# Rotary step of an attention kernel: one VectorE shuffle in place of four ScalarE copies

## The chip, the cores and the metric

The kernel runs on one core of a Trainium2 chip. The metric is the device time of one execution in microseconds (us). The core has five engines that run their own queues in order and wait for each other on semaphores: TensorE (PE in the profile, PEld its weight loads), VectorE (DVE), ScalarE (ACT), GpSimd (POOL) and SyncE (SP, which here only issues DMAs). Matmul results land in PSUM, in eight banks per partition; everything else lies in SBUF, 128 partitions wide.

## What is computed

A block with attention and a gated feed-forward part, in float32, for 4 sequences of 512 tokens and 1024 features. Cut to what the change touches, with the layer norm ahead of it:

```python
xn = _layernorm(x)
q = (xn @ Wq).reshape(b, s, 16, 64);  k = ...Wk;  v = ...Wv

def _rotate_every_two(x):
    r = jnp.stack((x[..., 1::2], x[..., ::2]), axis=-1)
    return r.reshape(x.shape)

def _apply_rotary(x, sin, cos):
    sin = jnp.repeat(sin[None, :, None, :], 2, axis=3)
    cos = jnp.repeat(cos[None, :, None, :], 2, axis=3)
    return x * cos + _rotate_every_two(x) * sin

logits = einsum(rotary(q), rotary(k)); causal mask; / sqrt(64); softmax; @ v; @ Wo
out = x + attention(xn) * silu(gated_ffn(xn))
```

The rotary step takes each pair of neighbouring features (2i, 2i+1), multiplies each by a cosine that the two share, and adds its partner times a sine that the two share. Both terms have a plus sign.

## The kernel before

The work goes by sequence b (0 to 3) and, within one, by group g (0 to 3) of four heads; a group has two units i of two heads each. Projections of queries and keys (m = 0, 1) for a group are made transposed, [128 partitions = two heads x 64 features, 512 tokens], by Strassen's scheme on halves: seven products of quarter matrices instead of eight. Each product is four matmuls of 128x256 into half a PSUM bank; `project_qk` collects them with ScalarE copies out of PSUM (L358, L387), VectorE sums out of PSUM (`add`, L352; the wide sum L389) and one GpSimd sum (L388). The result of a unit is the tile `c`. Values (m = 2) are projected by `project_v` (L425, L446, L451).

`rotary` (L313) is called one or two keys later, from inside the next projection. The host has sorted the columns of the weights so that, within a head, the 32 even features come first and the 32 odd ones after (L1388); the partner of partition p is then p + 32 or p - 32, in another block of 32 partitions. Four ScalarE copies (L319, L320) move the blocks to the tile `sw`, scaled by 0.125 for queries; VectorE makes `rot = c * sc * cos` (L321); GpSimd multiplies `sw` by the sine (L322) and adds the two (L323).

A group's attention is interleaved with the projections of the next group. `scores` (L525) writes two score tiles into a PSUM pool of their own and one (i = 1) into two banks of the shared ring; `softmax` adds the mask (L545), takes maxima (L548) on VectorE, exponentials on ScalarE (L551), reciprocals on VectorE (L559) and scales on GpSimd (L561). `transpose_blocks` transposes 32x32 blocks on VectorE (L579) and puts them in place with 16 DMAs from SyncE (L589). `values` multiplies by the values (L604), and ScalarE copies the result out of its bank (L613), which SyncE stores (L617).

The next sequence is loaded (`load_x`, L161), normalized on VectorE (L171 to L187), and transposed on TensorE: `transpose_x` makes two halves for each 128 tokens, and each half is copied out of PSUM by VectorE (L204) or ScalarE (L206). VectorE forms sums and differences of weights and of x for Strassen's scheme (`form_w` L288, `form_x` L303 and L311).

The ring is a PSUM pool of four banks that projections, the score tile i = 1, the values' products and the transposes of x share; a bank is free again when ScalarE or VectorE has read it out. The order of TensorE is the program's own, written out by hand; the order on the other engines is made by a planner from its own costs, in program order only where the code pins it. Behind the projections (from about 780 us) come the output projection (L1240) and the feed-forward part (L1011, L1180), which the change doesn't touch.

Of the kernel before, what the change touches and what calls it, by code (L numbers as in the profile page):

```python
# [11 lines left out]
AF = mybir.ActivationFunctionType  # L12
ALU = mybir.AluOpType
# [7 lines left out]
B, S, E = 4, 512, 1024  # L21
H, D = 16, 64
NE = 8
P = 128
# [4 lines left out]
TPB = S // P  # L29
# [4 lines left out]
SCALE = 0.125  # L34
# [2 lines left out]

QCOL = [0, P, 3 * P, 6 * P]
OFF = [0, 128, 256, 224]


@with_exitstack
def attn_gated_ffn_kernel(
# [15 lines left out]
    nc = tc.nc  # L59
# [13 lines left out]
        out=mask,  # L73
# [23 lines left out]
    for sign, base in ((1, 0), (-1, 7)):  # L97
        nc.gpsimd.affine_select(
            out=high,
# [42 lines left out]
    cos_sb = tabs.tile([P, S], F32, name="cos_sb")  # L142
    sin_sb = tabs.tile([P, S], F32, name="sin_sb")

    def bank(name):
        return ring.tile([P, S], F32, tag="r", name=name)

    def tp_bank(name):
        return bank(name).rearrange("p (t q) -> p t q", t=TPB)
# [44 lines left out]
    def transpose_x(b, t, g):  # L194
        if b not in X:
            X[b] = xp.tile([P, NC, S], F32, tag="X", name=f"X_{b}")
        tp = tp_bank(f"xtp_{b}_{t}_{g}")
        for j in range(4):
            c = 4 * g + j
            nc.tensor.transpose(tp[:, j, :], xin[b, t][:, c * P : (c + 1) * P], ident)  # L200
        dst = X[b][:, 4 * g : 4 * g + 4, t * P : (t + 1) * P]

        if (g == 0 and b > 0) or (g == 1 and (b, t) == (0, TPB - 1)):
            nc.vector.tensor_copy(dst, tp)  # L204
        else:
            nc.scalar.copy(dst, tp)  # L206
        if g == 1:

            queue = nc.scalar if (b, t) == (B - 1, TPB - 1) else nc.sync
            queue.dma_start(  # L210
                out=xn_d[b, t].rearrange("p (c q) -> p c q", c=NC),
                in_=X[b][:, :, t * P : (t + 1) * P],
            )
# [43 lines left out]
    def quarters_w(key):  # L257
        if key[2] < 2:
            w = W[key]
            return w[:, 0, :4, :], w[:, 0, 4:, :], w[:, 1, :4, :], w[:, 1, 4:, :]  # L260
        w, v = W[key, 0], W[key, 1]
        return w[:, :4, :], w[:, 4:, :], v[:, :4, :], v[:, 4:, :]

    def quarters_x(b):
        t = X[b]
        return t[:, :4, :TH], t[:, :4, TH:], t[:, 4:, :TH], t[:, 4:, TH:]
# [45 lines left out]

    def rotary(u, m, c):  # L313

        sc = SCALE if m == 0 else 1.0
        rot = qk.tile([P, S], F32, tag=f"rot{m}", name="rot%d_%d_%d_%d" % (m, *u))
        sw = tmp.tile([P, S], F32, tag="sw", name="sw%d_%d_%d_%d" % (m, *u))
        for r in range(0, P, 64):
            nc.scalar.activation(sw[r : r + 32, :], c[r + 32 : r + 64, :], AF.Copy, scale=sc)  # L319
            nc.scalar.activation(sw[r + 32 : r + 64, :], c[r : r + 32, :], AF.Copy, scale=sc)  # L320
        nc.vector.scalar_tensor_tensor(rot, c, sc, cos_sb, op0=ALU.mult, op1=ALU.mult)  # L321
        nc.gpsimd.tensor_tensor(sw, sw, sin_sb, op=ALU.mult)  # L322
        nc.gpsimd.tensor_tensor(rot, rot, sw, op=ALU.add)  # L323
        (Q, K)[m][u] = rot

    def project_qk(key):

        b, g, m = key
        pos = keys.index(key)
        after = keys[pos + 1] if pos + 1 < len(keys) else None  # L330
        a11, a12, a21, a22 = quarters_w(key)
        b11, b12, b21, b22 = quarters_x(b)
        un = "%d_%d_%d" % key
        c = [tmp.tile([P, S], F32, tag="c", name=f"c_{un}_{i}") for i in range(2)]

        def product(ps, wq, xq):
            for k in range(4):
                nc.tensor.matmul(  # L338
                    ps, lhsT=wq[:, k, :], rhs=xq[:, k, :], start=(k == 0), stop=(k == 3)
                )  # L340
                yield

        def halves(n):

            ps = bank(f"pj_{un}_{n}")
            return ps, ps[:, :TH], ps[:, TH:]

        def part(n):
            return tmp.tile([P, TH], F32, tag=f"part{n}", name=f"part_{un}_{n}", bufs=1)

        def add(out, ps, x):
            nc.vector.tensor_tensor(out, ps, x, op=ALU.add)  # L352

        _, p, r = halves(1)
        yield from product(p, a11, b11)
        yield from product(r, a12, b21)
        p1 = tmp.tile([P, S], F32, tag="part1", name=f"part_{un}_1", bufs=1)[:, :TH]
        nc.scalar.copy(p1, p)  # L358
        add(c[0][:, :TH], r, p1)
        if turn:  # L360
            rotary(*turn.pop(0))
        _, p, r = halves(2)
        yield from product(r, SF[key, 3], TF[b, 3])
        if pos == 0:

            bank3 = halves(3)
            yield from product(bank3[2], SF[key, 1], TF[b, 1])
        yield from product(p, SF[key, 2], TF[b, 2])
        u2, u3 = part(2), part(3)
        add(u2, p, p1)  # L370
        add(u3, r, u2)
        if turn:
            rotary(*turn.pop(0))
        if after:
            form_w(after, 3)
        if pos:
            ps, p, r = halves(3)
            yield from product(r, SF[key, 1], TF[b, 1])
        else:
            ps, p, r = bank3  # L380
        if after:
            form_w(after, 1)
            if after[2] < 2:
                form_w(after, 2)
        yield from product(p, a22, TF[b, 4])
        p5 = tmp.tile([P, S], F32, tag="part1", name=f"part_{un}_5", bufs=1)[:, :TH]
        nc.scalar.copy(p5, r)  # L387
        nc.gpsimd.tensor_tensor(u2, u2, p5, op=ALU.add)  # L388
        nc.vector.tensor_tensor(  # L389
            c[1].rearrange("p (h n) -> p h n", h=2),  # L390
            ps.rearrange("p (h n) -> p h n", h=2),
            u3[:, None, :].to_broadcast((P, 2, TH)),
            op=ALU.add,
        )
        load_w()
        _, p, _ = halves(4)
        yield from product(p, SF[key, 4], b22)
        add(c[0][:, TH:], p, u2)
        if after and after[2] < 2:
            form_w(after, 4)  # L400

        turn.extend([((b, g, i), m, c[i]) for i in range(2)])
        if m == 0:
            rotary(*turn.pop(0))
# [164 lines left out]
    def transpose_blocks(u, queues=(nc.sync,), ordered=False):  # L569
# [4 lines left out]
        for j in range(TPB):  # L574
            for i in range(j, TPB):
                src = probs(u, i)[:, :, j * P : (j + 1) * P]
                o = OFF[j] + 32 * (i - j)
                tc.keep_in_program_order(
# [17 lines left out]
    def values(u):  # L596
# [3 lines left out]
        for j in range(TPB):  # L600
            for h in range(2):
                r = h * D
                o = 320 * h + OFF[j]
                nc.tensor.matmul(  # L604
# [285 lines left out]
    for k, (b, g) in enumerate(groups):  # L890
# [38 lines left out]
        if k in (5, 9, 12, 14):  # L929
            n = {5: 0, 9: 2, 12: 4, 14: 6}[k]  # L930
# [121 lines left out]
    w, v = late  # L1052
# [318 lines left out]
def _rotary_tables():  # L1371
    f = np.float32
    inv = (f(1.0) / (f(10000.0) ** (np.arange(0, D, 2, dtype=f) / f(D)))).astype(f)
    ang = (np.arange(S, dtype=f)[None, :] * inv[:, None]).astype(f)
    return np.tile(np.cos(ang), (4, 1)).astype(f), np.tile(np.sin(ang), (4, 1)).astype(f)


# [49 lines left out]
```

## Time and profile before

| | |
|---|---|
| runs | 1107.7, 1110.0, 1110.5 us; median 1110.0 |
| span of the profiled execution | 1108.7 us, 15895 instructions |
| mean granted TensorE clock | 0.996 of full speed |
| ScalarE copies of the rotary step, L319 and L320 | 256, 628 ns each, 160.7 us |
| VectorE product L321 | 64, 734 ns mean, 45.3 us |
| GpSimd product and sum, L322 and L323 | 64 each, 1330 and 1419 ns mean |

A line of the timeline gives start and length in us, engine, line, operation, output and input tiles, how many alike in a row, and in brackets how long the engine had been idle before it and what it waited for. A line of a group gives busy us and the mean ns of one, then idle time before it and what ended that. "TensorE waits for ScalarE" means that its next matmul was released by a ScalarE instruction. Ends of matmuls are modelled, so neighbours overlap a little. The busy share by 40 slices of the span:

```
PE   9999999999999999999999999999999999999997
DVE  7888888788988978888887887887776877567663
ACT  2452754453375445427544452655530223122220
POOL 0772645555264555526453562675552433432334
```

### The profile page before, as it was taken

How to read it: one execution, taken by the hardware profiler on the slowest of the kernel's cores; microseconds unless marked ns; L12 is line 12 of the kernel's file. 1: busy time of each engine (PE TensorE's matmuls, PEld its weight loads, DVE VectorE, ACT ScalarE, POOL GpSimd, SP SyncE). 2: the span in 40 equal slices, each digit the busy share in tenths (PEclk: the TensorE clock that was granted, in tenths of full speed). 3: DMA queues.
4: the chain of work that ended last, by engine and by line, in shares of the span. 5: the costliest groups of instructions: out<-in, count | busy, mean ns of one | idle time of the engine just before them, and what ended most of it. 6: DMA issues, size and time to landing. Idle time of an engine off the chain costs nothing. (4 is left out here: it accounts for less than half of the span.)

```text
span 1108.7 us, 15895 instructions
## 1 busy us (share of the span) xinstructions
PE 1087.4 (98%) x5176; PEld 790.2 (71%) x5176; DVE 870.4 (79%) x1740; ACT 461.3 (42%) x1072; POOL 518.9 (47%) x566
## 2 busy tenths in 40 slices
PE   9999999999999999999999999999999999999997
PEld 8887778777777877777788687777664545654663
DVE  7888888788988978888887887887776877567663
ACT  2452754453375445427544452655530223122220
POOL 0772645555264555526453562675552433432334
PEclk9999999999999999999999999999999999999999
DMA  9415566544556654455666445544664222431331
GB/s 323 135 69 147 149 184 189 160 137 119 166 155 187 190 154 135 121 163 158 184 183 219 140 148 142 153 125 122 179 193 171 90 93 102 148 119 54 136 114 57
DMA packets 86770, 163.88 MB, mean 148 GB/s; under 512 B 13472, under 2 KB 49056, under 8 KB 80672
## 3 DMA queue, kind: packets, MB, share of 16 engines
q1 hardware_dynamic: 80144, 152.25, 46.1%
q0 software_dynamic: 4832, 9.05, 2.4%
q10 hardware_dynamic: 1712, 1.57, 0.5%
q8 instruction: 41, 0.67, 0.3%
q14 instruction: 41, 0.34, 0.1%
HBM read 95.45 MB, written 25.43 MB: 109 GB/s over the span
## 5 line engine op out<-in xcount | busy, mean ns | idle before, releaser
L561 POOL TENSOR_SCALAR p<-p,rs 128x256 f32<-128x256 f32 (+3 forms) x256 | 183.7, 734 | 200.6 <-DVE rs L559 136.2
L551 ACT ACTIVATE p<-sc,nmx 128x256 f32<-128x256 f32 (+3 forms) x256 | 132.9, 529 | 104.8 <-DVE nmx L548 87.2
L338 PE MATMUL pj<-X,w 128*128 128x256 f32 x576 | 134.3, 382 | 1.7 <-ACT p L551 1.5
L338 PE MATMUL pj<-T,S 128*128 128x256 f32 x512 | 120.5, 385 | 8.5 <-ACT v L613 8.5
L579 DVE STREAM_TRANSPOSE y<-p 128x256 f32<-128x256 f32 x320 | 112.4, 409 | 18.3 <-POOL p L561 16.9
L322 POOL TENSOR_TENSOR sw<-sw,sin_sb 128x512 f32<-128x512 f32 x64 | 85.1, 1330 | 81.1 <-ACT sw L320 75.4
L338 PEld LDWEIGHTS pj<-X,w 128*128 128x128 f32 x576 | 108.1, 190 | 20.0 <-issue 2.9
L338 PEld LDWEIGHTS pj<-T,S 128*128 128x128 f32 x512 | 96.7, 192 | 24.8 <-ACT v L613 11.3
L319 ACT ACTIVATE sw<-c 32x512 f32<-32x512 f32 x128 | 80.3, 628 | 70.0 <-DVE c L352 68.2
L338 PE MATMUL pj<-T,w 128*128 128x256 f32 x448 | 106.6, 382 | 0.0
L548 DVE TENSOR_REDUCE nmx<-sc 128x1 f32<-128x256 f32 (+3 forms) x160 | 105.2, 683 | 1.3
L425 PE MATMUL pj<-w,X 128*128 128x256 f32 x416 | 94.6, 380 | 0.8 <-ACT p L551 0.5
L338 PEld LDWEIGHTS pj<-T,w 128*128 128x128 f32 x448 | 83.4, 190 | 15.5 <-issue 4.6
L323 POOL TENSOR_TENSOR rot<-rot,sw 128x512 f32<-128x512 f32 x64 | 90.8, 1419 | 5.0
L425 PEld LDWEIGHTS pj<-w,X 128*128 128x128 f32 x416 | 78.2, 190 | 12.7 <-ACT p L551 2.0
L545 DVE TENSOR_TENSOR sc<-sc,mask 128x256 f32<-128x256 f32 (+1 forms) x160 | 57.0, 371 | 35.3 <-PE sc L525 35.3
L320 ACT ACTIVATE sw<-c 32x512 f32<-32x512 f32 x128 | 80.4, 628 | 1.6
L425 PE MATMUL pj<-w,T 128*128 128x256 f32 x352 | 80.2, 381 | 0.0
L525 PE MATMUL sc<-rot,rot 64*128 64x128 f32 (+3 forms) x512 | 79.7, 443 | 0.3 <-DVE v L451 0.3
L604 PE MATMUL pv<-p,v 128*64 128x256 f32 (+3 forms) x512 | 76.0, 439 | 0.4 <-issue 0.4
L388 POOL TENSOR_TENSOR part<-part,part 128x256 f32<-128x256 f32 x32 | 24.7, 771 | 105.2 <-ACT part L387 102.0
L613 ACT COPY v<-pv 128x512 f32<-128x512 f32 x32 | 18.7, 585 | 131.5 <-PE pv L604 131.4
(177 smaller groups left out, 1956.9 us busy)
## 6 DMA issues: line engine op xcount, KB each, us to landing
p<-y SPq DMA_DIRECT2D x496, 80.0 KB, 2.1
w<-in_wqk SPq DMA_DIRECT2D x31, 1024.0 KB, 5.3
w<-in_wv SPq DMA_DIRECT2D x16, 1024.0 KB, 5.2
x<-in_x SPq DMA_DIRECT2D x16, 512.0 KB, 4.3
at_d<-v SPq DMA_DIRECT2D x32, 256.0 KB, 2.7
xp<-xn_d SPq DMA_DIRECT2D x16, 512.0 KB, 4.6
ap<-at_d SPq DMA_DIRECT2D x16, 512.0 KB, 5.1
xr<-in_x SPq DMA_DIRECT2D x32, 256.0 KB, 3.0
```

The source lines that it names most:

```text
L319: nc.scalar.activation(sw[r : r + 32, :], c[r + 32 : r + 64, :], AF.Copy, scale=sc)
L320: nc.scalar.activation(sw[r + 32 : r + 64, :], c[r : r + 32, :], AF.Copy, scale=sc)
L322: nc.gpsimd.tensor_tensor(sw, sw, sin_sb, op=ALU.mult)
L323: nc.gpsimd.tensor_tensor(rot, rot, sw, op=ALU.add)
L338: nc.tensor.matmul(ps, lhsT=wq[:, k, :], rhs=xq[:, k, :], start=(k == 0), stop=(k == 3))
L425: nc.tensor.matmul(ps[:, j, :], lhsT=xq[:, k, j * P : (j + 1) * P], rhs=wq[:, k, :], start=(k == 0), stop=(k == 3),)
L525: nc.tensor.matmul(head(i, h), lhsT=Q[u][r : r + D, i * P : (i + 1) * P], rhs=K[u][r : r + D, : (i + 1) * P], start=True, stop=True,)
L548: nc.vector.tensor_reduce(nmx[:, hs], v, AX.X, ALU.max, negate=True)
L551: nc.scalar.activation(pt[:, h, :], ps[h], AF.Exp, bias=nmx[:, h : h + 1], accum_out=ssum[:, h : h + 1],)
L561: nc.gpsimd.tensor_scalar(pt[:, h, :], pt[:, h, :], rs[:, h : h + 1], 1.0, op0=ALU.mult, op1=ALU.mult,)
L579: nc.vector.transpose(out[:, :, :, o : o + 32], src.rearrange("p h (b c) -> p h b c", b=4))
L604: nc.tensor.matmul(by_block[r : r + D, :, 32 * j :], lhsT=V[u][:, j, r : r + D], rhs=PT[u][:, :, o : o + 32 * (TPB - j)], start=(j == 0), ...
```

## The change

The host no longer sorts the weights' columns: the partners lie in neighbouring partitions, 2i and 2i+1, and the tables of cosine and sine repeat each row twice. One VectorE `stream_shuffle` swaps neighbours within each block of 32 partitions, in place of the four ScalarE copies. The factor 0.125 of the queries is no longer applied in `rotary` but where the products are collected: the two ScalarE copies and the five VectorE sums of a query key take it along, and the plain product remains for the cosine. The first half of each transposed x tile of the sequences 1 to 3 is copied out of PSUM by ScalarE instead of VectorE.

```diff
+NEIGHBOUR = [n ^ 1 for n in range(32)]
...
-        if (g == 0 and b > 0) or (g == 1 and (b, t) == (0, TPB - 1)):
+        if g == 1 and (b, t) == (0, TPB - 1):
             nc.vector.tensor_copy(dst, tp)
         else:
             nc.scalar.copy(dst, tp)
...
     def rotary(u, m, c):
-        sc = SCALE if m == 0 else 1.0
...
-        for r in range(0, P, 64):
-            nc.scalar.activation(sw[r : r + 32, :], c[r + 32 : r + 64, :], AF.Copy, scale=sc)
-            nc.scalar.activation(sw[r + 32 : r + 64, :], c[r : r + 32, :], AF.Copy, scale=sc)
-        nc.vector.scalar_tensor_tensor(rot, c, sc, cos_sb, op0=ALU.mult, op1=ALU.mult)
+        nc.vector.stream_shuffle(sw, c, NEIGHBOUR)
+        nc.vector.tensor_tensor(rot, c, cos_sb, op=ALU.mult)
         nc.gpsimd.tensor_tensor(sw, sw, sin_sb, op=ALU.mult)
         nc.gpsimd.tensor_tensor(rot, rot, sw, op=ALU.add)
...
+        sc = SCALE if m == 0 else 1.0
+        def scaled_copy(out, ps):
+            if m == 0:
+                nc.scalar.activation(out, ps, AF.Copy, scale=sc)
+            else:
+                nc.scalar.copy(out, ps)
         def add(out, ps, x):
-            nc.vector.tensor_tensor(out, ps, x, op=ALU.add)
+            if m == 0:
+                nc.vector.scalar_tensor_tensor(out, ps, sc, x, op0=ALU.mult, op1=ALU.add)
+            else:
+                nc.vector.tensor_tensor(out, ps, x, op=ALU.add)
...
-        nc.scalar.copy(p1, p)
+        scaled_copy(p1, p)
...
-        nc.scalar.copy(p5, r)
+        scaled_copy(p5, r)
         nc.gpsimd.tensor_tensor(u2, u2, p5, op=ALU.add)
-        nc.vector.tensor_tensor(
+        add(
             c[1].rearrange("p (h n) -> p h n", h=2),
             ps.rearrange("p (h n) -> p h n", h=2),
             u3[:, None, :].to_broadcast((P, 2, TH)),
-            op=ALU.add,
         )
...
-    return np.tile(np.cos(ang), (4, 1)).astype(f), np.tile(np.sin(ang), (4, 1)).astype(f)
+    ang = np.tile(np.repeat(ang, 2, axis=0), (2, 1))
+    return np.cos(ang).astype(f), np.sin(ang).astype(f)
...
-        w = w.reshape(E, H, D // 2, 2).transpose(0, 1, 3, 2).reshape(E, E)
```

## The prediction

> **What bounds the kernel now.** I read the engines' busy times first, then who waits for whom, then the timelines around TensorE's waits, and last the groups that the edits touch.
>
> ```profile
> PE 1087.4 (98%) x5176; PEld 790.2 (71%) x5176; DVE 870.4 (79%) x1740; ACT 461.3 (42%) x1072; POOL 518.9 (47%) x566
> ```
>
> TensorE (PE) is busy in 1087.4 of 1108.7 us. The diff touches no matmul, and in the built changed program TensorE's instructions stand in the same order, so only the 21.3 us without a matmul, and stretches at a lowered clock, can move. Some of the 21.3 us are the start (1.5 us before the first matmul) and the tail behind the last one. In the middle, the waits view has for TensorE:
>
> ```profile
> PE pj L338 <- ACT v L613: 8.5, 7, 2.3
> ...
> PE pj L338 <- ACT p L551: 1.5, 2, 1.1
> PE pj L425 <- ACT p L551: 0.5, 1, 0.5
> ```
>
> Seven times, 8.5 us together, a projection waits for a PSUM bank that ScalarE has still to copy out (L613, the copy behind the values' matmuls). TensorE's timeline has them at 135.6, 233.5, 329.4, 427.1, 523.7, 623.5 and 720.6 us; three of the rows (start, length, what, in brackets the idle time before):
>
> ```profile
> 135.56 2.43 PE L338 MATMUL pj<-T,S 128*128 128x256 f32 x10 [1.20 <-ACT v L613]
> ...
> 427.07 3.72 PE L338 MATMUL pj<-T,S 128*128 128x256 f32 x16 [0.18 <-ACT v L613]
> ...
> 623.50 5.41 PE L338 MATMUL pj<-T,S 128*128 128x256 f32 x16 [2.34 <-ACT v L613]
> ```
>
> The last two rows hold the same sixteen records, yet one takes 5.41 and the other 3.72 us. The windows view (PE, PEld, DVE, ACT, POOL busy, then the granted clock) says why:
>
> ```profile
> 624.40:625.40 1.00, 1.00 (x5) 0.73 (x4) 0.14 (x1) 0.96 (x3) 0.61 (x1) 0.50 0.64 147
> ```
>
> After the 2.34 us wait the granted clock is 0.50 for some 3 us. After 1.81 us of waiting at 720.6 it stays at 1.00.
>
> Why is the copy late? ScalarE's timeline at the first wait:
>
> ```profile
> 129.78 0.63 ACT L319 ACTIVATE sw<-c 32x512 f32<-32x512 f32 x1 [4.02 <-DVE c L352]
> ...
> 134.28 0.62 ACT L320 ACTIVATE sw<-c 32x512 f32<-32x512 f32 x1
> 134.92 0.59 ACT L613 COPY v<-pv 128x512 f32<-128x512 f32 x1
> ```
>
> The values' matmuls end at 131.4 us, but eight rotary copies in a row (5.1 us) stand ahead of L613. At the other six, five to eight of them do.
>
> **The change, part by part.** The groups concerned (busy us, mean ns):
>
> ```profile
> L320 ACT ACTIVATE sw<-c 32x512 f32<-32x512 f32 x128 | 80.4, 628 | 1.6
> L319 ACT ACTIVATE sw<-c 32x512 f32<-32x512 f32 x128 | 80.3, 628 | 70.0 <-DVE c L352 68.2
> ...
> L579 DVE STREAM_TRANSPOSE y<-p 128x256 f32<-128x256 f32 x320 | 112.4, 409 | 18.3 <-POOL p L561 16.9 <-DMA w<-in_wqk 1.4
> L321 DVE SCALAR_TENSOR_TENSOR rot<-c,cos_sb 128x512 f32<-128x512 f32 x64 | 45.3, 734 | 0.2
> L389 DVE TENSOR_TENSOR c<-pj,part 128x512 f32<-128x512 f32 x32 | 21.9, 685 | 1.2
> L187 DVE TENSOR_SCALAR x<-x,mv,rstd 128x1024 f32<-128x1024 f32 x16 | 14.1, 885 | 0.1
> L204 DVE COPY X<-xtp 128x512 f32<-128x512 f32 x13 | 8.8, 680 | 1.6 <-PE xtp L200 1.2
> ```
>
> *Removed: 256 ScalarE copies*, 160.7 us. With them the seven waits go: L613 then runs when its matmuls end. That is -8.5 us, and -1.7 us (5.41 - 3.72) for the slow stretch behind the longest wait.
>
> The Trainium skill, "TensorE: Matmul & The Clock Gate", section "Why this matters for your kernels", asks only that idle gaps stay below about 3 us. By that rule the 2.34 us wait should not have lowered the clock, the 1.7 us would not be in the sum, and the time would come out 1.7 us higher; here the row has 0.50 after 2.34 us, and I follow the row.
>
> *Added: 64 shuffles on VectorE.* The trace has none. From below: L187 does 1024 elements a lane in 885 ns, so 512 in 0.44 us. From above: two L579 transposes of 256 elements, 0.82 us, and one more tiny instruction for the pattern if it needs one (the reciprocals of L559 take 0.16): 0.98. I take 0.68, the plain copy of the same shape in L204. So 64 x 0.68 = +43.5 us, 1.36 us for each pair of rotary steps (0.88 to 1.96).
>
> The skill's "VectorE: DVE Perf Modes", section "The perf-mode tier table (the rule you actually need)", speaks against the edit: the shuffle has no fast mode, about 2400 ns for 2048 elements against 2293 for a two-tensor operation. An estimate from that difference on top of 0.68 is 0.79 us a shuffle, some 0.2 us more per pair, and under 1 us more in the sum below.
>
> *Factor moved into the sums.* The PSUM sums become three-operand forms, L321 the plain product. The three-operand L321 is 0.68 us where nothing disturbs it (median 684 ns), the plain sum L389 0.685: no difference either way. The scaled ScalarE copies stay one instruction each.
>
> *Moved: 12 copies of L204 from VectorE to ScalarE* (the thirteenth stays): -8.2 us on VectorE, +12 x 0.584 = 7.0 on ScalarE, which keeps 461 - 161 + 7 = 307 us of work. Cover: ScalarE idles most of the span. The copies queue behind exponentials; one pair of those takes 1.3 us.
>
> *VectorE's net:* +43.5 - 8.2 = +35 us. Between 28 and 776 us it is busy in 626.9 of 748 us, so there is room on average; what counts is the queue at single places. Its timeline:
>
> ```profile
> 130.26 1.28 DVE L321 SCALAR_TENSOR_TENSOR rot<-c,cos_sb 128x512 f32<-128x512 f32 x2
> 132.48 0.43 DVE L545 TENSOR_TENSOR sc<-sc,mask 128x256 f32<-128x256 f32 x1 [0.93 <-PE sc L525]
> 133.34 0.72 DVE L545 TENSOR_TENSOR sc<-sc,mask 128x256 f32<-128x256 f32 x2 [0.43 <-PE sc L525]
> ...
> 620.27 1.28 DVE L321 SCALAR_TENSOR_TENSOR rot<-c,cos_sb 128x512 f32<-128x512 f32 x2
> 621.47 0.95 DVE L545 TENSOR_TENSOR sc<-sc,mask 128x256 f32<-128x256 f32 x3
> ```
>
> Behind a rotary pair stand the masks and maxima of the scores, and behind those the sum (L352) that frees the bank for the product after next. At 130 us the pair is followed by 0.93 + 0.43 us of waiting for TensorE, which swallow 1.36 us exactly; at 231 and 425 us that wait is 2.38. At 621 us there is none: maxima end at 624.54, then at 625.9, and the sum at 626.3. TensorE, no longer held, leaves its product at 621.2 and needs that bank 8 matmuls (3.46 us) later, at 624.6. So a new wait of 1.7 us: +1.7. From both sides: 0, if waits further up (1.31 us at 605.3 for an exponential behind rotary copies) shrink first; 2.9 plus a slow stretch of 1.7, so 4.6, if the shuffle is at its upper end and the pair before it isn't absorbed.
>
> Three places have no cover either: the scores at 156, 350 and 545 us, where VectorE has worked some 14 us without a break and TensorE is already held (0.48 us at 162.8). There a pair's 1.36 comes with one wait of 0.88 to absorb part (338.0, for an exponential) and a moved copy of 0.68. Two of them also take a later load: SyncE's order in the changed program has one x load behind sixteen p moves (10.84 us at 322.2), so it is issued at 333 rather than 318.8 and lands 4.3 us later at 337.4, where L171 reads it at 338.8. VectorE would wait if the transposes ahead slip by over 1.4. I take 0.7 us each, +2.1 (0 to 3 x 1.96 = 5.9).
>
> The waits of 0.37 and 1.12 us at 306.5 and 500.8 come from a late x load (VectorE waits 1.62 and 2.38 us for it), which soaks up a pair: 0 (-1.5 to +0.8).
>
> Sum: -8.5 - 1.7 + 1.7 + 2.1 = -6.4: span 1102.3. The median of the runs, 1110.0, stands 1.3 above the profiled span (the lowest run 1.0 below): 1103.6, forecast 1103.5. The bounds give a span of 1108.7 - 10.2 - 2.0 = 1096.5 and 1108.7 - 10.2 + 4.6 + 5.9 + 0.8 = 1109.8, with the 1.3 some 1098 and 1111.
>
> **The rivals.** *All of it is gained*: removing ScalarE's load also ends the small waits for exponentials (2.0 us), and VectorE's own waits for ScalarE and GpSimd (11.5 and 12.5 us at L352) shrink to make room: 1097.8. For it: at most places the cover is larger than the pair. Against: 621 us.
>
> *The waits only change hands*: each bank wait for ScalarE returns as one for VectorE, 8.5 to 11 us: 1110. For it: VectorE is the second busiest engine, at 90% in slices. Against: 231 and 425 us, with 2.38 us free.
>
> *Slower, by a dear shuffle.* VectorE's idle time between 28 and 776 us, 121.1 us, and the 8.2 freed, are used up when a shuffle costs (121.1 + 8.2) / 64 = 2.0 us. From there it decides: at the second scores of each of 16 groups a pair adds 4.0 us, the wait ahead covers about 1.3 (0 to 2.38 in the rows) and the bank is needed 1.1 us after it is free (235.5 against 236.6), so 1.6 x 16 = 26 us, less 10.2: 1125. For it: no row shows this operation. Against: L579 moves data between lanes too, and takes no longer than a sum of its size (409 against 418 ns in L352).
>
> **How the numbers follow.** 0.3% is what a measurement tells from no change here: 1106.7 to 1113.3. The forecast has 0.57, most of it (0.54) below 1106.7; all gained 0.15; hands changed 0.14, all within; slower 0.14. Faster 0.69, same 0.17, slower 0.14. The range runs from 1097 (just under all gained) to 1112.
>
> **What would show it.** ScalarE near 307 us; VectorE near 905; a shuffle row near 0.7 us; no wait of a projection for the values' copy; clock 1.00 at 624 us; small waits for VectorE or exponentials near 163, 356, 550 and 624 us. A shuffle above 1 us, or new TensorE waits of more than 6 us together, would prove me wrong.

## The result, and the profile after

The changed kernel takes 1124.0 us (median of four runs, 1120.5 to 1126.5) against 1109.2 us (1107.7 to 1110.5) before: a ratio of 1.0131, 95% interval 1.0114 to 1.0147. It is slower by 1.3%. The profiled execution spans 1124.8 us, 16.1 more than the one before.

The line of busy times (us, share of the span, instructions):

```profile
PE 1095.9 (97%) x5176; PEld 797.2 (71%) x5176; DVE 905.6 (81%) x1856; ACT 307.3 (27%) x828; POOL 524.0 (47%) x566
```

ScalarE is at 307 and VectorE at 905.6 us, where the prediction put them. TensorE's own busy time has grown by 8.5 us with the same matmuls. Some 5 us of that is a lowered clock: ahead of the tail the granted clock is 0.50 in five stretches of 3.41 us, against two before. Its waits (us in total, times, longest):

```profile
PE pj L433 <- ACT p L559: 5.2, 3, 1.7
PE sc L533 <- DVE v L459: 3.8, 3, 2.0
PE sc L533 <- DVE part L361: 2.8, 3, 1.6
PE pj L336 <- DVE part L361: 2.6, 1, 2.6
PE rt L678 <- DVE rex L674: 2.1, 1, 2.1
PE os L791 <- ACT p L559: 2.0, 1, 2.0
PE pj L336 <- ACT p L559: 1.7, 3, 0.7
```

The seven waits for the values' copy (now L621) are gone, every one. In their place TensorE waits for VectorE's sums (L361, L459), for the router's chain (L674), and for exponentials (L559) whose maxima VectorE made late. Laid matmul by matmul against before, TensorE gains 12 us at the seven old places (with the clock behind the longest), 1.2 at two small waits at 306 and 500 us, and loses 30 us elsewhere.

The groups of the rotary step, shapes apart (busy us, mean ns, then the idle time before and who ended it):

```profile
L587 DVE STREAM_TRANSPOSE y<-p 128x256 f32<-128x256 f32 x320 | 111.2, 407 | 24.8 <-POOL p L569 24.8
...
L320 POOL TENSOR_TENSOR sw<-sw,sin_sb 128x512 f32<-128x512 f32 x64 | 96.8, 1513 | 59.1 <-DVE sw L318 49.4 <-DVE mv L178 6.0 <-DVE rsum L659 2.4
...
L321 POOL TENSOR_TENSOR rot<-rot,sw 128x512 f32<-128x512 f32 x64 | 94.1, 1470 | 8.1 <-DVE rot L319 4.3
...
L319 DVE TENSOR_TENSOR rot<-c,cos_sb 128x512 f32<-128x512 f32 x64 | 63.4, 991 | 0.0
...
L318 DVE STREAM_SHUFFLE sw<-c 128x512 f32<-128x512 f32 x64 | 46.7, 730 | 0.0
```

The shuffle costs 730 ns, and its pattern load 12 ns more: near the 0.68 us assumed. But the cosine product beside it, the same size as before, went from 734 to 991 ns; GpSimd's sine product from 1330 to 1513 ns; and VectorE's transposes wait 24.8 us for GpSimd's scaled probabilities, where they waited 16.9.

What happens there is seen in the two engines' timelines just after the start, between 31 and 37 us (start, length; VectorE first, GpSimd's two rows last):

```profile
31.09 0.72 DVE L318 STREAM_SHUFFLE sw<-c 128x512 f32<-128x512 f32 x1
31.71 0.17 DVE L659 TENSOR_REDUCE rsum<-rex 128x4 f32<-128x32 f32 x1
31.79 0.68 DVE L319 TENSOR_TENSOR rot<-c,cos_sb 128x512 f32<-128x512 f32 x1
...
33.10 0.55 DVE L662 TENSOR_TENSOR rex<-rex,rrs 128x32 f32<-128x32 f32 x1
33.57 0.68 DVE L319 TENSOR_TENSOR rot<-c,cos_sb 128x512 f32<-128x512 f32 x1
34.18 1.24 DVE L667 CAST rhi<-rex 128x32 fp32r<-128x32 f32 x1
35.45 1.30 DVE L670 TENSOR_TENSOR rex<-rex,rhi 128x32 f32<-128x32 f32 x2
```

```profile
31.89 1.71 POOL L320 TENSOR_TENSOR sw<-sw,sin_sb 128x512 f32<-128x512 f32 x1 [2.41 <-DVE rsum L659]
33.68 1.70 POOL L321 TENSOR_TENSOR rot<-rot,sw 128x512 f32<-128x512 f32 x1
```

In before GpSimd's first rotary instruction stood at 33.45 us, behind four ScalarE copies, and the router's cast of 32 elements took 0.18 us:

```profile
32.29 0.18 DVE L659 CAST rhi<-rex 128x32 fp32r<-128x32 f32 x1
...
33.45 1.27 POOL L322 TENSOR_TENSOR sw<-sw,sin_sb 128x512 f32<-128x512 f32 x1 [4.51 <-ACT sw L320]
```

Now GpSimd is at work from 31.89 us, and the same cast takes 1.24 us: it ends at 35.42, when GpSimd's sum does (35.38). The pair of two-operand steps behind it takes 1.30 us against 0.29. The router is 2 us late, TensorE waits 2.07 us for it at 38.1 us and then has a stretch at half the clock.

GpSimd's queue has changed too. The planner, which sets the order there by its own costs, now puts rotary instructions ahead of the softmax's scaling that stood behind it. Around one scaling (the two of 128x128), before (first three lines) and after:

```profile
76.59 1.27 POOL L323 TENSOR_TENSOR rot<-rot,sw 128x512 f32<-128x512 f32 x1
77.84 0.72 POOL L561 TENSOR_SCALAR p<-p,rs 128x128 f32<-128x128 f32 x2
78.52 1.27 POOL L322 TENSOR_TENSOR sw<-sw,sin_sb 128x512 f32<-128x512 f32 x1
...
82.75 1.26 POOL L320 TENSOR_TENSOR sw<-sw,sin_sb 128x512 f32<-128x512 f32 x1
84.00 0.71 POOL L569 TENSOR_SCALAR p<-p,rs 128x128 f32<-128x128 f32 x2
84.68 1.27 POOL L321 TENSOR_TENSOR rot<-rot,sw 128x512 f32<-128x512 f32 x1
```

Of the 256 scalings, 38 have one or two rotary instructions more ahead of them than before.

### The profile page after: what moved, and what is told of

The parts are those of the page before. It is cut to its first block, busy times and chain, and to the rows that moved or that the text cites. A ratio compares the mean times of both kernels' runs of the same rounds, so it can differ in the third digit from the quotient of the medians.

```text
span 1124.8 us, 15775 instructions
## 1 busy us (share of the span) xinstructions
PE 1095.9 (97%) x5176; PEld 797.2 (71%) x5176; DVE 905.6 (81%) x1856; ACT 307.3 (27%) x828; POOL 524.0 (47%) x566
## 5 line engine op out<-in xcount | busy, mean ns | idle before, releaser
L569 POOL TENSOR_SCALAR p<-p,rs 128x256 f32<-128x256 f32 (+3 forms) x256 | 174.5, 697 | 212.9 <-DVE rs L567 133.7
L559 ACT ACTIVATE p<-sc,nmx 128x256 f32<-128x256 f32 (+3 forms) x256 | 132.6, 527 | 169.8 <-DVE nmx L556 125.6
L587 DVE STREAM_TRANSPOSE y<-p 128x256 f32<-128x256 f32 x320 | 111.2, 407 | 24.8 <-POOL p L569 24.8
L320 POOL TENSOR_TENSOR sw<-sw,sin_sb 128x512 f32<-128x512 f32 x64 | 96.8, 1513 | 59.1 <-DVE sw L318 49.4
L321 POOL TENSOR_TENSOR rot<-rot,sw 128x512 f32<-128x512 f32 x64 | 94.1, 1470 | 8.1 <-DVE rot L319 4.3
L533 PE MATMUL sc<-rot,rot 64*128 64x128 f32 (+3 forms) x512 | 84.0, 445 | 7.1 <-DVE v L459 3.8
L621 ACT COPY v<-pv 128x512 f32<-128x512 f32 x32 | 18.7, 585 | 205.8 <-PE pv L612 198.4
L433 PEld LDWEIGHTS pj<-w,T 128*128 128x128 f32 x352 | 67.2, 194 | 10.8 <-issue 2.0
L533 PEld LDWEIGHTS sc<-rot,rot 64*128 64x128 f32 x512 | 44.7, 187 | 39.4 <-issue 23.2
L553 DVE TENSOR_TENSOR sc<-sc,mask 128x256 f32<-128x256 f32 (+1 forms) x160 | 55.0, 368 | 17.7 <-PE sc L533 17.5
```

Source lines behind the costliest of these rows:

```text
L433: nc.tensor.matmul(ps[:, j, :], lhsT=xq[:, k, j * P : (j + 1) * P], rhs=wq[:, k, :], start=(k == 0), stop=(k == 3),)
L533: nc.tensor.matmul(head(i, h), lhsT=Q[u][r : r + D, i * P : (i + 1) * P], rhs=K[u][r : r + D, : (i + 1) * P], start=True, stop=True,)
L559: nc.scalar.activation(pt[:, h, :], ps[h], AF.Exp, bias=nmx[:, h : h + 1], accum_out=ssum[:, h : h + 1],)
L569: nc.gpsimd.tensor_scalar(pt[:, h, :], pt[:, h, :], rs[:, h : h + 1], 1.0, op0=ALU.mult, op1=ALU.mult,)
L587: nc.vector.transpose(out[:, :, :, o : o + 32], src.rearrange("p h (b c) -> p h b c", b=4))
```

## The experiments

Each kernel was measured beside the kernel before. Ratios are to that kernel, with 95% intervals; the last columns come from the profiles: VectorE's and GpSimd's busy time, the mean of the cosine product, and the transposes' wait for the scaled probabilities.

| kernel | us | ratio (95%) | VectorE us | GpSimd us | product ns | transposes wait us |
|---|---|---|---|---|---|---|
| before | 1109.2 | 1 | 870.4 | 518.9 | 734 | 16.9 |
| the change | 1124.0 | 1.0131 (1.0114-1.0147) | 905.6 | 524.0 | 991 | 24.8 |
| no sine product | 1098.4 | 0.9897 (0.9883-0.9912) | 889.1 | 427.8 | 897 | 7.1 |
| short read | 1102.6 | 0.9940 (0.9926-0.9955) | 887.7 | 485.0 | 823 | 12.1 |
| short write | 1108.0 | 0.9985 (0.9976-0.9995) | 891.1 | 483.8 | 883 | 12.6 |
| zeros for sine | 1120.2 | 1.0103 (1.0076-1.0130) | 896.5 | 532.5 | 761 | 15.0 |
| product first | 1111.6 | 1.0010 (0.9998-1.0022) | 897.7 | 518.9 | 774 | 16.4 |
| hop in place | 1125.5 | 1.0155 (1.0131-1.0178) | 907.1 | 517.2 | 1012 | 23.6 |
| hop, one buffer | 1135.0 | 1.0240 (1.0217-1.0262) | 909.0 | 516.0 | 1015 | 8.0 |
| no shuffle | 1134.4 | 1.0219 (1.0203-1.0234) | 887.5 | 531.9 | 1376 | 50.3 |
| cosine on GpSimd | 1132.0 | 1.0205 (1.0181-1.0230) | 859.5 | 594.2 | - | 68.0 |
| sine on VectorE | 1115.0 | 1.0056 (1.0037-1.0075) | 921.8 | 432.9 | 894 | 3.5 |
| all but the shuffle | 1107.3 | 0.9976 (0.9967-0.9986) | 857.4 | 517.6 | 734 | 19.3 |
| copies and shuffle | 1118.3 | 1.0080 (1.0063-1.0097) | 905.5 | 514.0 | 906 | 8.3 |
| scaling on ScalarE | 1117.4 | 1.0070 (1.0053-1.0086) | 893.8 | 352.8 | 949 | 0 |
| product first, scaling on ScalarE | 1111.5 | 1.0020 (1.0011-1.0030) | 882.0 | 342.7 | 740 | 0 |
| product first, half of it | 1109.4 | 1.0003 (0.9990-1.0016) | 895.0 | 435.7 | 764 | 8.8 |
| swap by DMA | 1153.4 | 1.0402 (1.0380-1.0424) | 858.4 | 530.1 | 916 | 1.9 |
| before, values' copy on VectorE | 1106.2 | 0.9972 (0.9963-0.9981) | 886.3 | 521.4 | 737 | 18.2 |
| all but the shuffle, values' copy on VectorE | 1105.3 | 0.9967 (0.9954-0.9981) | 873.0 | 520.3 | 733 | 19.3 |

### Is it the shuffle, or GpSimd beside it?

Theory B was that the shuffles' own time makes VectorE late; theory A, that GpSimd's sine product, which now starts right behind the shuffle, does. First the sine product alone is taken out:

```diff
-        nc.gpsimd.tensor_tensor(sw, sw, sin_sb, op=ALU.mult)
```

> The changed kernel without GpSimd's sine product (the swapped values are summed as they are, so the output lacks the sines); the order of every other instruction is that of the changed kernel on VectorE, ScalarE and TensorE. Theory A (GpSimd's sine product, which now starts right behind the shuffle, makes VectorE's work beside it longer): the cosine product falls from a mean of 991 ns to 0.68 to 0.75 us, VectorE's busy time from 905.6 to 880 to 890 us, the pair of shuffles costs 1.4 us again and not 2.0, and of the roughly 25 us of new TensorE waits and low clock at least a third goes: 1110 to 1117 us. Theory B (the shuffles' own 46.7 us alone make masks, maxima and sums late): the cosine product stays near 0.99 us, VectorE within 3 us of 905.6, time 1122 to 1126 us.

Measured 1098.4 us, lower than either theory had it. All 64 shuffles are there, in the same order. The busy times and TensorE's waits of this run:

```profile
PE 1082.7 (99%) x5176; PEld 788.8 (72%) x5176; DVE 889.1 (81%) x1856; ACT 308.4 (28%) x828; POOL 427.8 (39%) x502
```

```profile
PE pj L433 <- ACT p L559: 3.2, 3, 1.4
...
PE rt L678 <- DVE rex L674: 0.6, 1, 0.6
```

The router's wait falls from 2.1 to 0.6 us, the waits for L459 go. VectorE issues the same instructions in the same order as in the change, yet spends 16.5 us less in them and 17.7 us less waiting for GpSimd's probabilities. ScalarE, GpSimd (but for the products) and the DMAs keep their order as well, so the planner has no part in this difference. With the sine product away the shuffles are affordable: the time is near that of the rival "all of it is gained" (1097.8), in a run that also spares GpSimd 96 us. The product did not fall to 0.7 us, though: it now meets GpSimd's scaling (886 ns in 19 cases) and GpSimd's sum (1250 ns in 14), since the first product's sum runs while the second product does.

The order of the two VectorE instructions, turned:

```diff
-        nc.vector.stream_shuffle(sw, c, NEIGHBOUR)
         nc.vector.tensor_tensor(rot, c, cos_sb, op=ALU.mult)
+        nc.vector.stream_shuffle(sw, c, NEIGHBOUR)
```

> The changed kernel with the cosine product ahead of the shuffle; the same instructions, the output is unchanged. Theory A (collision with GpSimd's sine product): the first cosine product of a pair has no sine product of its own beside it, the second still runs beside the first's, so the mean falls from 991 to about 0.70 to 0.85 us, VectorE's busy time by 9 to 18 us; what now stands beside the sine product instead (forms, masks) gives some of it back; time 1113 to 1121 us. Theory B (queue length by the shuffles alone): product 0.99 us, time 1122 to 1126 us.

1111.6 us, and the product at 774 ns: 12.4 of the 14.8 us of loss go when the two neighbours are turned. That is not the turn alone: the planner answered it with another order on GpSimd, where 40 of the 256 scalings now have one rotary instruction fewer ahead of them. And without the shuffle:

```diff
-        nc.vector.stream_shuffle(sw, c, NEIGHBOUR)
-        nc.gpsimd.tensor_tensor(sw, sw, sin_sb, op=ALU.mult)
+        nc.gpsimd.tensor_tensor(sw, c, sin_sb, op=ALU.mult)
```

> The changed kernel without the shuffle; GpSimd's sine product reads the unswapped projection, so the output has the wrong partners. Theory B (the shuffles' own time): all new waits go and the seven waits for the values' copy stay away: VectorE near 840 us with the product at 0.70 us, time 1097 to 1101 us. Theory A (collision): the sine product starts together with the cosine product, which stays at 0.9 to 1.3 us; the pair costs 0.5 to 1 us over before where it cost 2.0, time 1101 to 1110 us.

Both theories missed: 1134.4 us, slower than the change, with 46.7 us of work taken from VectorE. The product's row among the groups, and the transposes' among VectorE's waits:

```profile
L319 DVE TENSOR_TENSOR rot<-c,cos_sb 128x512 f32<-128x512 f32 x64 | 86.6, 1376 | 0.2
```

```profile
DVE y L587 <- POOL p L569: 50.3, 15, 6.6
```

Sine and cosine product are now ready at the same moment. The cosine product takes 1376 ns in the mean, and GpSimd's rotary holds up the scaling of the probabilities: before the transposes at 83.13 us, for one, two rotary sums (2.50 us) run ahead of the last scaling, and VectorE has waited 6.61 us (3.93 in before). All such waits make 50.3 us.

### Are the other parts of the change neutral?

```diff
-        nc.vector.stream_shuffle(sw, c, NEIGHBOUR)
+        for r in range(0, P, 64):
+            nc.scalar.copy(sw[r : r + 32, :], c[r + 32 : r + 64, :])
+            nc.scalar.copy(sw[r + 32 : r + 64, :], c[r : r + 32, :])
```

> The changed kernel with four ScalarE copies in place of the shuffle, and tables and columns in the order of before: what is left of the change is the factor in the sums and the twelve copies of X on ScalarE. If these parts are neutral: the time of before, 1107 to 1112 us, the waits of projections for the values' copy back (about 8 us), product 0.68 to 0.74 us. If the moved copies of X or the scaled sums carry the loss (theory C): 1115 us or more, with waits behind ScalarE's queue that is now 12 copies longer.

1107.3 us, a little below before. The factor in the sums and the moved copies of X do no harm; theory C falls. The whole loss comes with the shuffle in place of the four copies.

### A lock between the engines, or GpSimd's queue?

Two ways were left for the sine product: VectorE's instructions with two SBUF operands can't run beside a GpSimd read (A1), or GpSimd's time itself is what comes ahead of the scaling (A2). Instead of the sine product, GpSimd writes zeros:

```diff
-        nc.gpsimd.tensor_tensor(sw, sw, sin_sb, op=ALU.mult)
+        nc.gpsimd.memset(sw.bitcast(mybir.dt.uint8), 0)
```

> The changed kernel in which GpSimd, in the place of the sine product and behind the same shuffle, writes zeros over the swapped tile byte by byte (2048 bytes a partition, by the rows of its other memsets, 204 ns for 128 and 301 ns for 256 elements, about 1.6 us each), so the output lacks the sine part; GpSimd is as busy as with the product but reads nothing from SBUF. It parts the two ways in which the sine product can cost. Theory A1 (what costs is that VectorE's work with two SBUF inputs can't run beside a GpSimd instruction that reads SBUF): product near that of the run without the sine product (897 ns, what is left is the sums), forms shorter, time 1098 to 1106 us. Theory A2 (what costs is GpSimd's own queue: the rotary stands ahead of the softmax's scaling and VectorE's transposes wait for it, 24.8 us in the changed kernel and 7.1 us without the sine product): the transposes' wait stays above 20 us and the time at 1115 to 1126 us.

The writes took 1811 ns each. The product fell to 761 ns (the 55 that met no GpSimd two-tensor instruction have a median of 678), so a write does not hold it up; yet the time is 1120.2 us. It is not a clean test: the planner's order differs a little on VectorE and GpSimd, and the router's cast, 0.18 us in before, takes 1.66 beside such a write and ends with it. So two instructions of nearly equal length in the sine product's place, one that reads (first line) and one that only writes (second):

```diff
+        nc.gpsimd.tensor_scalar(sw, sw, 1.0, 1.0, op0=ALU.mult, op1=ALU.mult)
+        nc.gpsimd.memset(sw.bitcast(mybir.dt.bfloat16), 0.0)
```

> The changed kernel with GpSimd's sine product replaced by a multiplication of the swapped tile by 1 (one SBUF input; the output lacks the sines); by the scaling's row for the same shape 0.76 to 0.88 us each, so GpSimd is about 45 us less busy than in the changed kernel. VectorE's order is that of the changed kernel. Theory A1 (reads of GpSimd hold up VectorE's work with two SBUF inputs): product 0.85 to 0.95 us, 3 us or more slower than the run that writes for as long: 1106 to 1113 us. Theory A2 (GpSimd's queue): as the run that writes, within 2 us.

> The same with GpSimd writing zeros over the swapped tile instead (as 1024 two-byte elements, about 0.9 us each by the rows of 1811 ns for 2048, 301 for 256; nothing is read; the output lacks the sine part). Theory A1: product 0.75 us, time 1099 to 1105 us, 3 us or more below the run that reads. Theory A2: the same time as the run that reads, within 2 us, both between the 1098.4 us without the sine product and the 1120.2 us with writes of 1.8 us.

Their rows on GpSimd, the read first:

```profile
L320 POOL TENSOR_SCALAR sw<-sw 128x512 f32<-128x512 f32 x64 | 56.3, 880 | 60.1 <-DVE sw L318 49.9 <-DVE mv L178 6.4 <-DVE rsum L659 2.4
```

```profile
L320 POOL MEMSET sw<- 128x1024 bf16 x64 | 60.8, 951 | 56.3 <-DVE sw L318 52.6 <-DVE rsum L659 2.4 <-DVE rs L567 1.3
```

The run that reads is the faster one, 1102.6 against 1108.0 us, where A1 asked for the reverse. The pair does not rule the lock out, though, because it hardly varied it. In each run 17 products meet the read or the write alone, and take 667 and 668 ns. What holds products up in both is GpSimd's sum: those that meet the sum as well take 1158 ns beside the read (6 cases) and 1410 beside the write (12). In the write run nine of GpSimd's instructions also stand in another order. Neither does A2 get its "within 2 us".

What holds is a dose. The run without the product, the short read and the change have the same order on every engine; with 0, 0.88 (one operand read) and 1.51 us (two) of GpSimd between shuffle and sum they take 1098.4, 1102.6 and 1124.0 us. The two writes, in slightly different orders, take 1108.0 (0.95 us) and 1120.2 (1.81 us). GpSimd's time in that place is what costs; how much of it is the lock and how much the queue isn't parted by these runs.

### Does the earlier start matter?

```diff
+        nc.scalar.copy(sw, sw)
         nc.gpsimd.tensor_tensor(sw, sw, sin_sb, op=ALU.mult)
```

> The changed kernel with one ScalarE copy of the shuffled tile onto itself between the shuffle and the sine product (output unchanged; no buffer more, so ScalarE waits for the shuffle alone). Theory A3 (an early start of the sine product is what costs): product 0.70 to 0.90 us, waits for GpSimd's scaling no longer than in the changed kernel, time 1106 to 1116 us. If the start does not matter, but the work does: 1121 to 1127 us. Rival: the hop makes ScalarE wait behind shuffles as it did behind copies and the values' copy is late again, 1124 us or more.

1125.5 us. With a start that is one ScalarE copy (620 ns) later, the product is still at 1012 ns, where A3 asked for 0.70 to 0.90, and the transposes' wait is 23.6 us for 24.8. The time itself is no clean answer: as in the rival, the values' copy is late again (4.4 us in two of TensorE's waits). An earlier form of the same test had a tile of its own for the copy, with one buffer:

> The changed kernel with one ScalarE copy of the shuffled tile between the shuffle and GpSimd's sine product (output unchanged): the work of VectorE and GpSimd is the same, the sine product starts 0.6 to 1.5 us later, ScalarE gets 64 copies of about 0.6 us (to about 345 us). Theory A (the loss comes from when the sine product starts: right behind the shuffle, beside the cosine product and ahead of the softmax's scaling): cosine product from 991 to 0.70 to 0.85 us, time 1105 to 1114 us, like the run with the product first. Theory B' (GpSimd's and VectorE's loads decide, wherever the sine product starts): 1120 to 1126 us.

It came out at 1135.0 us and tells little: ScalarE waited 86.6 us for GpSimd to free that buffer, and the values' copy was late again (11.2 us). A3, that an early start as such costs, is not borne out by the products; what the start is worth in time stays open.

### VectorE's load and GpSimd's rotary together

The next runs set the load apart from the place. The four ScalarE copies stay, and a shuffle whose result nobody reads is added:

```diff
+        nc.vector.stream_shuffle(off, c, NEIGHBOUR)
         for r in range(0, P, 64):
             nc.scalar.copy(sw[r : r + 32, :], c[r + 32 : r + 64, :])
             nc.scalar.copy(sw[r + 32 : r + 64, :], c[r : r + 32, :])
```

> The kernel with the four ScalarE copies and the rest of the change (1107.3 us measured), plus one shuffle of each projection tile into a scratch tile that nobody reads: VectorE gets the changed kernel's 46.7 us of shuffles, while GpSimd's sine product still waits for ScalarE's copies; output unchanged. Theory C1 (VectorE's load and GpSimd's rotary work together make the loss, in whatever order they stand): 1116 to 1126 us, product 0.8 us or more. Theory C2 (it is the place of the sine product directly behind the shuffle): 1107 to 1112 us, product 0.73 to 0.80 us.

1118.3 us, 11.0 above the same kernel without it; theory C1. TensorE's waits in this run:

```profile
PE pj L340 <- ACT v L625: 4.9, 3, 2.2
PE pj L340 <- DVE c L365: 4.5, 3, 1.6
PE sc L537 <- DVE v L463: 3.2, 3, 1.1
PE pj L437 <- ACT p L563: 3.1, 3, 1.1
```

Waits for VectorE (L365, L463) come on top of those for ScalarE: 4.5 and 3.2 us, where the same kernel without the shuffle has 2.4 and 0.3. With the sine product in GpSimd's queue, even behind ScalarE's copies, 46.5 us of shuffles cost 11 us. What they would cost without the sine product isn't measured, since no kernel with neither was run. The other way round, the sine product given to VectorE:

```diff
-        nc.gpsimd.tensor_tensor(sw, sw, sin_sb, op=ALU.mult)
+        nc.vector.tensor_tensor(sw, sw, sin_sb, op=ALU.mult)
```

> The changed kernel with the sine product on VectorE, GpSimd keeps the sum alone (output unchanged): VectorE gets 64 times about 0.69 us more (to 930 to 940 us), GpSimd 428 us as in the run without the product. Theory C1' (GpSimd's time between shuffle and sum, and what it does to VectorE, decides): below the changed kernel, 1105 to 1116 us. Theory B (VectorE's queue alone decides): its longest load of all, 1126 us or more.

1115.0 us, 9 below the change with the longest VectorE queue of all (921.8 us). Theory B, VectorE's queue alone, falls here. And the reverse load, the cosine product on GpSimd:

```diff
-        nc.vector.tensor_tensor(rot, c, cos_sb, op=ALU.mult)
+        nc.gpsimd.tensor_tensor(rot, c, cos_sb, op=ALU.mult)
```

> The changed kernel with the cosine product on GpSimd too (shuffle on VectorE, both products and the sum on GpSimd; output unchanged): VectorE loses 63 us of work and goes to 835 to 850 us, below before; GpSimd gains 64 times 1.3 to 1.5 us and goes to 610 to 625 us. If VectorE's load sets the new waits: 1098 to 1105 us. If GpSimd's queue and the forms beside its reads set them (theories A1 and A2): the transposes' wait for GpSimd goes from 24.8 to 40 us or more, forms S from 845 ns to 900 or more, time 1120 to 1140 us.

1132.0 us with VectorE at 859.5, below before: the transposes wait 68.0 us for GpSimd. So a loss needs no added load on VectorE.

### Looking for a version that beats both

> The changed kernel with the softmax's scaling by the reciprocal sums on ScalarE, which the change has made idle, and not on GpSimd (output unchanged): GpSimd loses 174 us (to about 350 us), ScalarE gets 256 scalings of 0.4 to 0.6 us (to 410 to 460 us). Theory A2 (GpSimd's queue makes VectorE's transposes late): their wait for the scaling falls below 10 us, time 1098 to 1108 us although the cosine product still meets the sine product (0.9 us or more). Rival: ScalarE's queue, where a scaling waits for VectorE's reciprocal with the next exponentials and the values' copy behind it, gives it back: 1112 to 1125 us, with projections and scores that wait for p or for the values' copy.

> The same move of the softmax's scaling to ScalarE, with the cosine product ahead of the shuffle as well (output unchanged). If the two causes add (beside the product, A1, and in GpSimd's queue, A2): 1097 to 1103 us, below the kernel before. If ScalarE's queue becomes the limit: 1108 to 1120 us.

> Product ahead of the shuffle, and of the softmax's scaling one head of two on ScalarE and the other on GpSimd (output unchanged): GpSimd near 430 us, ScalarE near 370 us. If ScalarE's queue was what held the full move back at 1111.5 us (4.9 us at one wait for the gate's split, 4.5 us for exponentials), half of it leaves more than half of the gain: 1101 to 1107 us. If the waits for exponentials stay: 1108 to 1113 us.

```diff
-                nc.gpsimd.tensor_scalar(pt[:, h, :], pt[:, h, :], rs[:, h : h + 1], 1.0, op0=ALU.mult, op1=ALU.mult)
+                nc.scalar.activation(pt[:, h, :], pt[:, h, :], AF.Copy, scale=rs[:, h : h + 1])
```

With the scaling on ScalarE the transposes' wait for it is gone, but TensorE waits 7.2 us for exponentials and 4.9 us in one wait behind the attention stage: 1117.4, and with the product first 1111.5 us. With one head of two there: 1109.4 us, no different from before. None beats it.

The swap by four DMAs a tile needs neither ScalarE nor the shuffle:

> Neither shuffle nor ScalarE copies: four DMAs of 64 KB from SyncE's queue swap the halves of each projection tile (tables and columns in the order of before; factor in the sums; output unchanged). The sine product starts 2 to 3 us after the projection's last sum, as in before, so it meets the cosine product no more (product 0.69 to 0.76 us), VectorE 855 to 862 us, ScalarE near 308 us, and the projections' waits for the values' copy stay away. If nothing else is late: 1098 to 1103 us. Rival: SyncE's queue is in order, 256 more issues stand ahead of the moves of the transposed probabilities, each waiting for a projection's sum; the values' matmuls wait for those moves: 1108 to 1120 us, with waits of the values for DMA.

1153.4 us. The DMAs land 3.5 us (median) after issue, GpSimd waits 120 us for them, and the weights' loads on the same queue land after 6.4 us instead of 5.3.

What did work is to leave the rotary where it was and take the values' copy out of ScalarE's queue:

```diff
         at = V[u]
-        nc.scalar.copy(
+        nc.vector.tensor_copy(
```

> The kernel before with one change only: the copy of the values' result out of PSUM on VectorE and not on ScalarE, so that it no longer queues behind the rotary's copies (output unchanged). VectorE gets 32 times about 0.5 us, 16 us spread over the attention stage. If the gain that the change was meant to have (8.5 us of waits and 1.7 us of low clock) is to be had without the shuffle: 1098 to 1103 us. If VectorE's queue makes the bank as late as ScalarE's did: 1107 to 1113 us, with projections that wait for VectorE's copy.

> No shuffle: the four ScalarE copies with the factor in the sums and the copies of X on ScalarE (1107.3 us measured), and the values' copy on VectorE (which alone gave 1106.2 us in the kernel before); output unchanged. If the gains add: 1102 to 1105 us. If they are the same gain twice (both only take the projections' wait for the values' copy): 1105.5 to 1108 us.

1106.2 us in the kernel before, 1105.3 us with the neutral parts of the change: 0.3% faster than before, intervals under 1. The gain expected of the change is only partly there; its longest wait (2.34 us, with the low clock) goes, but others come: 1.8 us for VectorE's copy, 3.7 more for exponentials, and one of 2.1 for a DMA.

## Why the prediction was wrong

*Right.* The seven waits are gone (12 us won with the clock, 10.2 forecast); the shuffle is 730 ns for an assumed 680; ScalarE is at 307 us; the factor in the sums changes nothing (419 ns a sum with it, 418 before). That VectorE's 905.6 us fit is luck: the cosine products took 18.1 us that the prediction didn't have, and other work gave it back, the weight forms alone 11 us (154 in before, 143 now).

*Wrong: "1.36 us for each pair of rotary steps".* It came from the shuffles alone. The step before it priced the plain product with "no difference either way", but in the changed kernel the product takes 991 ns. A pair costs 2 x 0.73 for the shuffles and 2 x 0.26 for the longer products: 2.0 us. This is the step that failed first. It compared the instruction with itself and didn't ask what GpSimd does at that moment: the four removed copies had also kept GpSimd's sine product some 2.5 us behind.

*That price could be read in the trace of before.* Put beside GpSimd's records, the weight forms of L288 of 512 elements and two SBUF operands (S from w) take 677 ns in the 42 cases that meet no GpSimd instruction, and 1180 ns in the 15 that overlap one of its two-tensor instructions. The cosine product takes 683 ns in 32 undisturbed cases and 785 ns in the 32 that overlap other GpSimd work, mostly the scaling. The PSUM sums of L352 take 412 ns alone and 410 beside one. Two such forms, and the sine product that the second one meets:

```profile
27.43 0.68 DVE L288 TENSOR_TENSOR S<-w 128x512 f32<-128x512 f32 x1
...
37.56 1.22 DVE L288 TENSOR_TENSOR S<-w 128x512 f32<-128x512 f32 x1
...
36.51 1.72 POOL L322 TENSOR_TENSOR sw<-sw,sin_sb 128x512 f32<-128x512 f32 x1
```

The Trainium skill says the same in "SBUF — State Buffer", section "Who interferes with whom": a VectorE instruction with two SBUF inputs and a GpSimd instruction that reads SBUF exclude each other, and the one that starts second waits. The rows agree for the products (678 ns alone, 1019 beside a GpSimd two-tensor instruction, in the changed kernel) and for the shuffle with its one operand (725 alone, 732 beside). They agree on who waits, too: of the 18 products that meet only a sine product, 17 started ahead of it and take at most 685 ns; the 21 that meet a sum as well take 1151 ns.

*Wrong: the new waits, "+1.7" and "+2.1".* At the scores near 156, 350 and 545 us the loss is 7.9 us for 2.1, at 612 to 629 us 2.9 for 1.7. (The "8 matmuls (3.46 us)" of the second sum are sixteen, the x16 row at 623.50; the time is right for sixteen.) The rest, some 19 us, is at places that the prediction didn't look at, because TensorE had little to wait for there before: the router at 31 to 38 us (4.0 with the clock), the first units' transposes and sums at 79 to 92 us (3.4), 278 and 472 us, and 640 to 820 us. It searched for lost cover only behind the pair's next instructions on VectorE, not in the loop through GpSimd: VectorE's late reciprocals make the scaling late, the scaling the transposes, and these stand ahead of the sums. In the change VectorE loses 34 us against the same instructions without the sine product, 16.5 in them and 17.7 before its transposes.

*The rivals.* "Slower, by a dear shuffle" had the sign and the wrong mechanism: the shuffle is far from the 2.0 us at which it was to decide, and that its 1125 us is so near the measured 1124.0 is luck. The time of "all of it is gained" comes out when GpSimd's sine product is away.

*Shown, and open.* Shown: the loss hangs on GpSimd's sine product behind the shuffle. With every engine's order kept, the loss becomes a gain when a shorter instruction that reads one operand stands there, and a larger one when none does. Shown too: 46.5 us of shuffles added to the rotary of copies cost 11 us, and with no work added to VectorE, GpSimd's rotary work can cost more than the change does (no shuffle, cosine on GpSimd). Open: the shares of the lock, of GpSimd's queue and of the planner's order in it; and why a write of 1.81 us costs a little less than a product of 1.51.

## What to carry to other kernels

When work moves off an engine that was slow, ask what its slowness held back: the next step starts earlier, on another engine, beside other work. Price two engines that feed each other as one loop, and take the price of an instruction from its records beside the neighbour it will have, not from its mean. And try the order of two independent neighbours before judging a change; here it was worth 12 us, with the order that the planner then gave GpSimd.

## What the runs showed of the hardware

A 12 ns pattern load and 730 ns for a shuffle of 512 fp32 elements, whether GpSimd works beside it or not; a cast of 32 elements that takes 0.18 us alone and 1.66 beside a GpSimd write; a sum of 256 elements with one operand in PSUM that GpSimd's work leaves as it is (412 ns alone, 410 beside a two-tensor instruction, in before).

The clock goes by a grid. The low stretches in the records, but for the last of each run, are 3.41 us long or twice that, and their starts lie on a grid of that period. Summing TensorE's idle time in each cell, in before the cells with 2.34 and 2.01 us are followed by a cell at 0.50, and none with 1.39 or less; in the change 2.07, 1.98, 2.04 and 1.87 are, two with 1.73 are not. With the product first there are waits of 2.31 and 2.17 us without a lowered clock: the grid cuts them into 1.18 + 1.13 and 0.53 + 1.64. So in these runs the same wait costs 1.7 us more or nothing, by where it falls. Over all profiles there are exceptions both ways (1.98 without, 1.16 with), and the second cell of the change's one double stretch follows a cell with 0.1 us of idle time. In the windows view (PE, PEld, DVE, ACT, POOL busy, granted clock, DMA share, GB/s) of the change, two stretches of full work, behind a wait of 2.07 and one of 1.73 us:

```profile
38.60:41.60 3.00, 3.00 (x8) 2.36 (x7) 2.32 (x6) 0.00 (x0) 0.00 (x0) 0.50 0.07 16
172.00:175.00 3.00, 3.00 (x16) 2.64 (x15) 1.02 (x3) 2.50 (x9) 2.27 (x5) 1.00 0.56 126
```

Eight matmuls in the one, sixteen in the other.
